# Splitting attention's weights into 16-bit planes: from VectorE to ScalarE

## The chip, the cores and the metric

The kernel runs on one core of a Trainium2 chip. A core has five engines with a queue of instructions each, which run side by side and wait for one another by semaphores: TensorE (PE, with its weight loads shown apart as PEld), VectorE (DVE), ScalarE (ACT), GpSimd (POOL) and SyncE (SP, which here only issues transfers). The metric is the device time of one execution in microseconds (us); of several executions the median is given.

## The reference

The input x holds 128 graphs of 64 nodes with 512 features in float32, and adj is one 64 x 64 mask for all of them. Four layers follow one another, each of the form x = x + f(relu(layernorm(x))):

```python
h = relu(layernorm(x)); x = x + mha0(h, adj)            # q, k, v with bias; 8 heads of 64
h = relu(layernorm(x)); x = x + mha1(h, adj) @ Wo + bo  # the same, with an output projection
h = relu(layernorm(x)); x = x + rel(h, adj)             # (adj.T * q k^T), rows scaled to norm 1, times v
h = relu(layernorm(x)); o = mha3(h, adj) @ Wp + bp      # no biases on q, k, v
x = x + o + layernorm(o) * gamma + beta
```

In mha the scores q k^T / 8 are masked, go through a softmax over the neighbours j, and weight the values. Layer 2 has no softmax.

## The kernel before

**Tiles.** 512 rows of x (8 graphs) make a tile, four blocks of 128 rows. There are 16 tiles in each layer, 64 in all, numbered n; layer l = n // 16. A tile's rows are loaded (`load_x`), normalised (`layer_norm`, line 516), and turned, so that features stand on the partitions (`hT`). The projections to q, k, v and the output are Strassen-like block products (`projection`, line 630): seven products of 256 x 256 blocks instead of eight, in the order 1, 6, 5, 2, 7, 3, 4 (line 44), where the fourth is split once more for some weights. Product 2 goes into the bank of product 1, product 7 into that of 6, product 3 into that of 5 (line 645). Sums of the inputs are made on POOL, sums of the results on POOL and DVE, and copies out of the matmul banks (PSUM, 8 of them) on ACT: the first copy of each projection is `s<-mm`, of product 1; `z<-mm` is product 5.

**Attention** of a tile (`attend`, line 813), in two halves g: after the k projection PE makes the scores (`begin_scores`), DVE adds the mask (`s`) and reduces the maximum (`mx`), POOL subtracts it, ACT takes the exponential in place, DVE sums (`sr`) and inverts, POOL multiplies. The weights are then turned, two blocks of 128 x 512 for each half, so four turns for a tile. The value products (`values`) follow while the next tile's q and k projections are under way. The last tile's weights are turned on PE instead.

**A turn** (`turn`, line 505). A float32 block [...] is split into two planes: all low halves of the 512 floats of a row, then all high halves, as 1024 uint16 (`z<-s` for attention's weights, `z<-xin` for the normalised rows; from six buffers). SP issues a transposing transfer (`hp<-z`, five buffers), and a copy on ACT puts the halves together again in their turned place (`s<-hp`, `hT<-hp`). Three places call it: line 481 for a weight (4 times), line 554 for the normalised rows (252), line 836 for attention's weights (4 for each of 47 tiles: 188). The split is on DVE (line 509), the copy back on ACT (line 514).

**The order of the work** isn't that of the program text. Every operation is recorded as a step with an engine, the steps it depends on, a duration booked by `duration` (line 265) and a delay until others see its result. `Plan.order` (line 150) then builds each engine's queue greedily: of the steps that are ready on the engine that is free first, it takes the one with the lowest rank, which is the place in the text, less 100 (`RUSH`) where the step reads a matmul bank; the score and value products come ahead. A 16-bit copy is booked at 0.67 ns for each element on DVE (line 284), after which POOL may not start until it is over, and which itself waits until POOL is free (lines 192 and 199); on ACT it is booked at 1.32 ns for each element (line 290) without regard to POOL. Each queue is issued in that order (line 217, so all instructions carry that line in the profile) and runs in order on the chip.

Of the kernel before, what the change touches and what calls it, by code (L numbers as in the profile page):

```python
# [13 lines left out]
U16 = mybir.dt.uint16  # L14
# [7 lines left out]
KC = D // P  # L22
# [279 lines left out]
def gnn_stack_kernel(  # L302
# [12 lines left out]
    pe, dve, act, gps = plan.tensor, plan.vector, plan.scalar, plan.gpsimd  # L315
# [143 lines left out]
    def fold():  # L459

        rq = yield from raw("oT", wq2, "rq")
        rk = yield from raw("SO", wk2, "rk")
        yield 4
        for dc in range(KC):
            while not mm.free:
                yield 1
            pa = mm.take("fold")
            plan.begin()
            for ec in range(KC):
                pe.matmul(pa, rq[:, ec, ts(dc, P)], rk[:, ec, :], start=(ec == 0), stop=(ec == KC - 1))  # L470
            plan.end()
            f = zs.tile([P, D], F32, tag="z", name=f"fa_{dc}")
            act.copy(f, pa)
            mm.give("fold")
            dma(a2d[dc * P : (dc + 1) * P, :], f)
            yield 1
        rv = yield from raw("oT", wv2, "rv")
        yield 4
        for ec in range(KC):
            f = zs.tile([P, KC, P], F32, tag="z", name=f"ft_{ec}")  # L480
            turn(f, rv[:, ec, :], f"v2_{ec}")
            dma(v2d.rearrange("(c p) e -> p c e", p=P)[:, :, ts(ec, P)], f)
            yield 6
# [18 lines left out]
    l_of = lambda n: n // NB  # L502
    ready = set()

    def turn(dst, src, nm):


        zp = zs.tile([P, D], F32, tag="z", name=f"zp_{nm}").bitcast(U16).rearrange("p (w f) -> p w f", w=2)
        dve.tensor_copy(zp, src.bitcast(U16).rearrange("p (f w) -> p w f", w=2))
        hp = hps.tile([P, 2, KC, P], U16, tag="hp", name=f"hp_{nm}")  # L510
        plan.sync.dma_start(
            hp.rearrange("p w c t -> p (w c) t"), zp.rearrange("p w f -> p (w f)"), transpose=True
        )
        act.copy(dst.bitcast(U16).rearrange("p c (t w) -> p w c t", w=2), hp)

    def layer_norm(n):
# [34 lines left out]
        for t in range(NT) if n else ():  # L551
            z = xins[n][t]
            act.activation(z, z, AF.Relu, bias=nb[:, t : t + 1], scale=rs[:, t : t + 1])
            turn(hT[:, :, ts(t, P)], z, f"{n}_{t}")
            yield 1
# [228 lines left out]
    def begin_scores(n, qT, kT):  # L784
        first = len(plan.steps)
        psss = scores(qT, kT, n)
        plan.join(first, 300)
        spawn(attend(n, take_scores(n, psss)))
# [24 lines left out]
    def attend(n, ss):  # L813
        for s in ss:
            sf = s.rearrange("p q b j -> p (q b) j")
            mx = sm.tile([P, NS], F32, tag="mx", name=f"mx_{n}")
            dve.tensor_reduce(mx, sf, AX.X, ALU.max)
            gps.tensor_tensor(sf, sf, mx.unsqueeze(2).to_broadcast([P, NS, G]), ALU.subtract)
            yield 1
        yield 1  # L820
        for s in ss:
            sf = s.rearrange("p q b j -> p (q b) j")
            act.activation(sf, sf, AF.Exp, scale=QS)
            sr = sm.tile([P, NS], F32, tag="sr", name=f"sr_{n}")
            dve.tensor_reduce(sr, sf, AX.X, ALU.add)
            dve.reciprocal(sr, sr)
            gps.tensor_tensor(sf, sf, sr.unsqueeze(2).to_broadcast([P, NS, G]), ALU.mult)
            yield 1

        aTs = []  # L830
        for s in ss:
            aT = s.rearrange("p (q c) b j -> p q c (b j)", q=2)
            aTs.append(aT)
            for p in range(2):
                if n < N - 1:
                    turn(aT[:, p], s[:, p * KC : (p + 1) * KC].rearrange("p c b j -> p (c b j)"), f"a_{n}_{p}")
                else:
                    pt = blocks(mm.take("last"))
                    plan.begin()
                    for c in range(KC):  # L840
                        pe.transpose(pt[:, c, :], s[:, p * KC + c].rearrange("p b j -> p (b j)"), ident)
                    plan.end()
                    act.copy(aT[:, p], pt)
                    mm.give("last")
                yield 1
        due.append((n, aTs, vs[n]))
        ready.add(("a", n))
# [410 lines left out]
    for t in range(NT):  # L1258
        ps = mm.take("last")
        plan.begin()  # L1260
        for j in range(2):
            for kc in range(KC):
                w = ((W["o3"][:, W11], w12), (W["o3"][:, W21], W["o3"][:, W22]))[kc // 2][j]
# [51 lines left out]
```

## Time and profile before

| | |
|---|---|
| median of 3 runs | 2834.38 us (2831.71 to 2835.23) |
| profiled execution | 2832.0 us, span 2829.9 us |
| PE busy | 2803.2 us, 99% |
| DVE busy | 1999.9 us, 71% |
| ACT busy | 1318.5 us, 47% |
| POOL busy | 2138.8 us, 76% |
| split of attention's weights, DVE | 188 x 1218 ns |
| split of the normalised rows, DVE | 252 x 976 ns |
| copy back to attention's weights, ACT | 188 x 1350 ns |

The span runs from the first to the last instruction of the profiled execution; the time of that execution has some 2 us more around it. A row of the groups names what is written and read (`z<-s`), the shape, the count, the busy time in all and the mean of one, and then the time for which the engine stood idle before such instructions, with what ended it. A releaser is inferred from semaphores. In the timeline a line is a start, a length and an instruction, with its idle time before in brackets; "x3" are three in a row.

### The profile page before, as it was taken

The numbers are of one execution on the slowest core, as the hardware profiler recorded it, in microseconds if no ns is written. First come the engines' busy times: TensorE is split into PE (matmuls) and PEld (weight loads), VectorE is DVE, ScalarE is ACT, GpSimd is POOL, SyncE is SP. The second block draws the span as 40 slices with busy tenths as digits, with TensorE's granted clock in tenths as the row PEclk, the third lists the DMA queues.
The fourth block names the chain that finished last, engine by engine and source line by source line (L and its number), as shares of the span: only waits on it lengthen the run. The fifth ranks groups of instructions, "written<-read, shape, count | busy, mean of one in ns | idle before, by whom it ended". The sixth has DMA issues, their size and how long they took to land.

```text
span 2829.9 us, 65896 instructions
## 1 busy us (share of the span) xinstructions
PE 2803.2 (99%) x26787; PEld 2481.2 (88%) x26787; DVE 1999.9 (71%) x3549; ACT 1318.5 (47%) x1907; POOL 2138.8 (76%) x2089
## 2 busy tenths in 40 slices
PE   9999999999999999999999999999999999999998
PEld 8888788888888888888888888888888888888887
DVE  7777667777766767767765665655588777877776
ACT  4455545445554454444543444444444444444441
POOL 6656565668898888888889655566778788788785
PEclk9999999999999999999999999999999999999999
DMA  6676556567452443443454766656656656766754
GB/s 155 133 158 148 131 152 161 114 131 165 112 128 76 105 119 77 105 120 79 106 144 114 172 156 154 160 140 164 135 113 137 145 138 141 150 135 138 161 112 117
DMA packets 645520, 375.03 MB, mean 133 GB/s; under 512 B 485728, under 2 KB 566880, under 8 KB 643296
## 3 DMA queue, kind: packets, MB, share of 16 engines
q1 hardware_dynamic: 634608, 338.32, 50.4%
q0 software_dynamic: 10608, 32.51, 6.3%
q8 instruction: 209, 3.42, 0.5%
q14 instruction: 95, 0.78, 0.1%
HBM read 152.61 MB, written 69.21 MB: 78 GB/s over the span
## 4 chain that ended last, share of the span: by engine, by line
PE 93%; POOL 3%; DMA 1%; DVE 1%; issue 1%; ACT 0%; POOLq 0%; SPq 0%; ACTq 0%; DVEq 0%
PE mm L217 93%; DMA hp<-z 1%; POOL S L217 1%; POOL w L217 1%; DMA xo<-w 0%; POOL s L217 0%; POOL xo L217 0%; POOL SO L217 0%; POOL u L217 0%; DVE xo L217 0%; DVE z L217 0%; DMA xin<-in_x_dram 0%; DVE st L217 0%; ACT s L217 0%; DVE w L217 0%
## 5 line engine op out<-in xcount | busy, mean ns | idle before, releaser
L217 PE MATMUL mm<-S,w 128*128 128x256 f32 x3584 | 812.0, 379 | 1.9 <-ACT z L217 1.9
L217 PEld LDWEIGHTS mm<-S,w 128*128 128x128 f32 x3584 | 679.3, 190 | 95.4 <-ACT z L217 2.5
L217 PE MATMUL mm<-hT,w 128*128 128x256 f32 (+1 forms) x3040 | 612.2, 347 | 2.9 <-ACT q L217 1.9
L217 PEld LDWEIGHTS mm<-hT,w 128*128 128x128 f32 x3040 | 506.9, 191 | 59.9 <-ACT q L217 2.7
L217 DVE TENSOR_TENSOR u<-mm,s 128x512 f32<-128x512 f32 x414 | 284.2, 687 | 300.9 <-PE mm L217 238.8
L217 PE MATMUL mm<-w,S 128*128 128x256 f32 x2048 | 472.4, 381 | 2.0 <-DVE u L217 2.0
L217 PEld LDWEIGHTS mm<-w,S 128*128 128x128 f32 x2048 | 384.6, 190 | 55.6 <-DVE u L217 2.4
L217 ACT COPY hT<-hp 128x1024 uint16<-128x1024 uint16 x252 | 332.5, 1351 | 49.3 <-DMA hp<-z 49.0
L217 PE MATMUL mm<-w,hT 128*128 128x256 f32 (+1 forms) x1696 | 349.2, 347 | 0.7 <-ACT s L217 0.7
L217 ACT COPY s<-hp 128x1024 uint16<-128x1024 uint16 x188 | 250.2, 1350 | 172.2 <-DMA hp<-z 109.8
L217 POOL TENSOR_TENSOR s<-s,mx 128x1024 f32<-128x1024 f32 x96 | 181.7, 1917 | 193.8 <-DVE mx L217 190.9
L217 PEld LDWEIGHTS mm<-w,hT 128*128 128x128 f32 x1696 | 285.2, 191 | 32.7 <-ACT s L217 1.1
L217 ACT COPY s<-mm 128x512 f32<-128x512 f32 x211 | 123.0, 584 | 376.3 <-PE mm L217 187.2
L217 DVE COPY z<-s 128x1024 uint16<-128x1024 uint16 x188 | 225.0, 1218 | 64.7 <-POOL s L217 64.6
L217 DVE COPY z<-xin 128x1024 uint16<-128x1024 uint16 x252 | 240.1, 976 | 20.2 <-ACT xin L217 16.7
L217 PE MATMUL mm<-w,SO 128*128 128x256 f32 x992 | 225.0, 379 | 1.0 <-POOL SO L217 1.0
L217 ACT ACTIVATE xin<-xin,nb,rs 128x512 f32<-128x512 f32 x256 | 194.5, 810 | 64.1 <-DVE nb L217 64.0
L217 POOL TENSOR_TENSOR xo<-xo,row 128x512 f32<-128x512 f32 x128 | 169.1, 1340 | 66.2 <-DMA xo<-in_x_dram 66.2
L217 PEld LDWEIGHTS mm<-w,SO 128*128 128x128 f32 x992 | 188.2, 190 | 26.9 <-POOL SO L217 1.2
L217 POOL TENSOR_TENSOR qT<-u,z 128x512 f32<-128x512 f32 x64 | 90.4, 1412 | 144.8 <-DVE u L217 124.7
L217 POOL TENSOR_TENSOR u<-u,q 128x128 f32<-128x128 f32 (+1 forms) x256 | 175.3, 693 | 30.4 <-DVE q L217 22.7
L217 POOL TENSOR_TENSOR s<-s,sr 128x1024 f32<-128x1024 f32 x96 | 188.5, 1972 | 7.7 <-DVE v L217 3.6
(125 smaller groups left out, 4245.1 us busy)
## 6 DMA issues: line engine op xcount, KB each, us to landing
xin<-x SPq DMA_DIRECT2D x192, 256.0 KB, 3.5
xo<-x SPq DMA_DIRECT2D x64, 512.0 KB, 6.1
xin<-in_x_dram SPq DMA_DIRECT2D x64, 256.0 KB, 4.2
x<-xo SPq DMA_DIRECT2D x64, 256.0 KB, 2.5
x<-xo SPq DMA_DIRECT2D x128, 128.0 KB, 2.7
x<-xo SPq DMA_DIRECT2D x32, 512.0 KB, 3.2
xo<-row POOLq DMA_DIRECT2D x16, 1024.0 KB, 8.1
out_dram<-xo SPq DMA_DIRECT2D x30, 512.0 KB, 2.8
```

What stands on the lines that cost most here:

```text
L217: getattr(getattr(self.nc, eng), op)(*a, **k)
```

## The change

`turn` gets a parameter for the operation that splits, with DVE's copy as its default. Attention's call hands in ACT's copy. The other two callers keep DVE. What the split reads and writes is the same. Since the queues are built from all booked durations, every engine's order is made anew.

```diff
-    def turn(dst, src, nm):
+    def turn(dst, src, nm, split=dve.tensor_copy):
 
 
         zp = zs.tile([P, D], F32, tag="z", name=f"zp_{nm}").bitcast(U16).rearrange("p (w f) -> p w f", w=2)
-        dve.tensor_copy(zp, src.bitcast(U16).rearrange("p (f w) -> p w f", w=2))
+        split(zp, src.bitcast(U16).rearrange("p (f w) -> p w f", w=2))
...
                 if n < N - 1:
-                    turn(aT[:, p], s[:, p * KC : (p + 1) * KC].rearrange("p c b j -> p (c b j)"), f"a_{n}_{p}")
+                    turn(aT[:, p], s[:, p * KC : (p + 1) * KC].rearrange("p c b j -> p (c b j)"), f"a_{n}_{p}", act.copy)
```

## The prediction

> **What bounds the kernel now.** I read the busy shares and the chain that ended last first, since they say which engine's time is the time.
>
> ```profile
> PE 2803.2 (99%) x26787; PEld 2481.2 (88%) x26787; DVE 1999.9 (71%) x3549; ACT 1318.5 (47%) x1907; POOL 2138.8 (76%) x2089
> PE 93%; POOL 3%; DMA 1%; DVE 1%; issue 1%; ACT 0%; POOLq 0%; SPq 0%; ACTq 0%; DVEq 0%
> ```
>
> TensorE (PE) works 2803.2 of the 2829.9 us span and is 93% of the chain. Matmul busy time alone could deceive, so I checked the floor: in the timeline eight 128x256 matmul records stand 1.73 us apart from the next eight, 216 ns each, the same in every quiet stretch. The change takes away no matmul, so those 2803.2 us stay. What can move is the 26.7 us in which PE is idle. The third view cuts the span at the places where the chain leaves PE:
>
> ```profile
> core 0: us, PE busy (x) PEld busy (x) DVE busy (x) ACT busy (x) POOL busy (x), PEclk, DMA share, GB/s
> 0.00:720.00 720.00, 715.77 (x7202) 621.34 (x7203) 520.59 (x835) 365.43 (x476) 449.79 (x348) 1.00 0.64 145
> 720.00:1470.00 750.00, 747.37 (x7264) 667.69 (x7263) 529.30 (x893) 353.63 (x539) 659.40 (x655) 1.00 0.42 104
> 1470.00:1570.00 100.00, 94.89 (x845) 83.03 (x845) 57.16 (x97) 37.59 (x56) 95.94 (x107) 1.00 0.53 133
> ...
> 2020.00:2060.00 40.00, 37.34 (x423) 32.72 (x423) 17.35 (x32) 17.00 (x25) 24.98 (x30) 1.00 0.61 118
> ...
> 2785.00:2830.00 45.00, 32.86 (x286) 28.96 (x284) 31.50 (x56) 7.36 (x14) 22.45 (x24) 0.93 0.38 94
> ```
>
> Stretch less PE busy: 4.2 us idle up to 720 (3.5 of it in the first 50 us), 2.6 at the border from layer 0 to 1, 5.1 from layer 1 to 2, 2.7 from layer 2 to 3, 12.1 at the end (span end 2829.9). The two stretches left out have none. Start and end aside, 11.1 us of PE idle can be won in the whole kernel, and POOL at 96% busy is what holds 1470 to 1570.
>
> Now the operation itself, its nearest relatives, and who waits in front of it:
>
> ```profile
> L217 ACT COPY s<-hp 128x1024 uint16<-128x1024 uint16 x188 | 250.2, 1350 | 172.2 <-DMA hp<-z 109.8
> L217 DVE COPY z<-s 128x1024 uint16<-128x1024 uint16 x188 | 225.0, 1218 | 64.7 <-POOL s L217 64.6
> L217 DVE COPY z<-s x188: 631/1042/2387, 53.5 to 2750.1; 128x1024 uint16<-128x1024 uint16 x188
> ACT z L217 <- PE mm L217: 277.0, 135, 5.1
> DVE z L217 <- POOL s L217: 64.6, 25, 4.2
> ```
>
> The split (z<-s) takes 631 ns at best and 1218 in the mean: the rest is spent inside the instruction. The last two lines are waits (us in total, times, longest): DVE stood 25 times for POOL's normalised weights, while ACT's waits are mostly for PE's own products.
>
> [...] copies of 631 ns and of 2387 ns are the same shape, and in the timeline a copy begun at 724.11 ends at 726.49, 0.6 us after POOL's multiplication (to 725.9). [...] The split on ACT isn't in this trace: I [...] take 1.35, the same engine, type and size.
>
> **The change part by part.**
>
> *Removed from DVE:* 188 copies (47 tiles x 4), 225.0 us. DVE falls from 1999.9 to about 1775 us (63%). It is not the bound, and it waits for PE 238.8 us ahead of the u adds alone, so this is worth nothing by itself.
>
> *Added to ACT:* 188 x 1.35 = 254 us; ACT rises to 1572 us (56%). In layer 0 it is densest: 365 + 64 x 1.35 = 452 of 720 us, 63%. [...] Cost at nothing in throughput: the cover is ACT's 1511 us of idle time.
>
> *The attention chain:* weights wait for split, transpose DMA, un-split on ACT, then the value products. The split gets 1.35 - 1.22 = 0.13 us longer each. In the tile around 770 us the second normalisation ends at 769.9; four ACT splits from 767.2 back to back end at 772.6, where DVE ended its fourth at 772.4. Eight ACT copies in a row would end at 778.0, 779 with the PSUM evacuations between them; before, the last un-split ended at 779.0 and PE took up the value products at 782.5. So 3.5 us of cover remains: nothing.
>
> *Evacuations behind splits on ACT:* this is the new wait. ACT is in order, and behind a split may stand the copy s<-mm or z<-mm that empties a PSUM bank. In the new order built from the changed kernel 73 of the 188 splits are followed directly by a PSUM reader, 63 by another split, 44 by an un-split, 8 by the layer norm. The cover: products 6 and 5 run between product 1 and product 2, which reuses its bank, 2 x 1.73 us; less the 0.58 us copy leaves 2.9 us of allowed delay. One split (1.35) or two (2.70) are hidden; two with a wait for POOL between them are not. I book 1 us in the whole kernel for such cases, between nothing and the rival below.
>
> [...] POOL no longer meets these copies. Layer 0 to 1 border:
>
> ```profile
> 724.11 4.90 DVE L217 COPY z<-s 128x1024 uint16<-128x1024 uint16 x3 [2.76 <-POOL s L217]
> 725.89 1.71 POOL L217 TENSOR_TENSOR v<-u,z 128x512 f32<-128x512 f32 x1
> 727.63 0.84 ACT L217 ACTIVATE z<-mm,bq 128x256 f32<-128x256 f32 x2 [4.12 <-POOL v L217]
> 728.53 1.99 PE L217 MATMUL mm<-S,w 128*128 128x256 f32 x8 [1.91 <-ACT z L217]
> ```
>
> POOL's v add takes 1.71 instead of 1.27 (the same form unhindered) under a split; ACT's z waits for it, PE for z. That is 0.44 us of the 1.91. At the 1 to 2 border, between 1501 and 1510 us, POOL runs a pair of w adds in 3.09 (free: 2.54), an xo add in 1.72, a u add and an xo add in 1.60 each (free: 1.27): 0.55 + 0.45 + 0.33 + 0.33 = 1.66 us, on the chain that holds PE there. Sum: 2.1 us won if all of it reaches PE. Elsewhere in layers 0, 1 and 3 the relief meets a PE that doesn't wait: nothing.
>
> *Moved:* the greedy planner re-sorts every queue. In the new PE order the groups that run after a later-recorded one fall from 261 to 234 of 1866 (from 43 to 30 at the 1 to 2 border, but up in layer 3, from 18, 6, 8, 6, 6, 7, 12 to 21, 10, 12, 11, 9, 13, 10 per twenty-fourth of the recorded products). On SP's queue the transposes and the next tile's xin loads swap places; xin is loaded a tile ahead, so a swap of a few 1.3 us issues is covered. The ACT instructions of the change are copies as they stand there already, and one activation table load is all the trace has, at 3.6 us. The first 65 entries of PE's order are unchanged, so the start's 3.5 us stay. At the end POOL's and DVE's lists differ by swaps of one or two instructions; the last DMA add still lands before the last four output tiles: within 1 us either way.
>
> *Sum:* +1.0 - 0.44 - 1.66 = -1.1 us. The profiled execution before took 2832.0 us (2829.9 span and 2.1 around it); that gives 2830.9. The median of the runs, 2834.38, lies 2.4 above the profiled one, so the forecast for it is 2833.3.
>
> **The rivals.**
>
> A, slower: ACT becomes a queue with a blocked head. The 25 waits for POOL's weights (64.6 us, 2.6 each, 4.2 at most) move from DVE to ACT, where every PSUM copy stands behind. 2.6 + 1.35 = 3.95 us against 2.9 of cover leaves 1.07 us of PE idle each; all 25 give 27 us, half of them 13 us: 2848. It decides from 6 of the 25 (5.7 us). For it: ACT makes the first copy of every projection, and layer 3's PE order has more late groups. Against it: DVE's u adds stood behind the same waits, and PE lost nothing outside the borders.
>
> B, faster: [...] Both vanish, 2.6 + 5.1 = 7.7 us: 2826.7. For it: POOL at 96% there, and fewer late groups in the new order. Against it: most of that 100 us is POOL's own work, which stays.
>
> C, the change does nothing because the order puts the splits on ACT only in name: excluded, all 188 stand on ACT in the built program, and VectorE's count falls by 188.
>
> **How the numbers follow.** 0.2% (5.7 us) is about what a measurement of this kernel can tell from no change. Likeliest, hidden either way, 2833.3: 0.60, its own range 2829 to 2839. A: 0.30, anywhere from 2840 to 2861, centre 2848. B: 0.10, 2824 to 2828. Faster, same, slower: 0.10, 0.60, 0.30. The range 2827 to 2850 leaves out about half of B and under half of A.
>
> **What would show it.** PE busy within 2 us of 2803; the row z<-s on ACT at 1.35 us [...]; DVE near 1775 and ACT near 1570 us; z<-xin on DVE still stretched, [...]; POOL's v, xo and w adds nearer 1.27. ACT should show a wait of z for POOL's s, some tens of us. I am wrong if PE idles outside the borders for more than 6 us with ACT's s, z or q as releaser (rival A), or if the border stalls, under 5 us together, show that B held.

## The result and the profile after

The changed kernel takes 2855.06 us (median, 2854.29 to 2855.71) against 2834.38: a ratio of 1.0074, interval 1.0057 to 1.0092. It is slower by about 21 us. The profiled execution has a span of 2853.9 us, before 2829.9.

First the busy times of after:

```profile
PE 2816.4 (99%) x26787; PEld 2490.4 (87%) x26787; DVE 1805.6 (63%) x3361; ACT 1488.2 (52%) x2095; POOL 2076.8 (73%) x2089
```

DVE gave up 194 us, POOL 62 us, ACT took 170 us. PE has the same 26787 matmuls, and yet 13.2 us more of busy time. That is the first hint: the same work took longer on an engine that the change doesn't touch. (The chain of waits is of no use here. In this execution it breaks off after 2% of the span, so I read stretches and waits instead.)

Next the same stretches as in the prediction, of after; the first column is the stretch, then its length, then the busy time and instructions of each engine, then PE's granted clock:

```profile
core 0: us, PE busy (x) PEld busy (x) DVE busy (x) ACT busy (x) POOL busy (x), PEclk, DMA share, GB/s
0.00:720.00 720.00, 717.60 (x7207) 623.69 (x7208) 458.88 (x772) 423.50 (x540) 431.83 (x352) 1.00 0.62 145
720.00:1470.00 750.00, 743.25 (x7228) 663.50 (x7228) 453.31 (x830) 407.67 (x594) 624.11 (x647) 1.00 0.42 103
1470.00:1570.00 100.00, 97.58 (x833) 85.82 (x834) 50.83 (x97) 41.07 (x63) 97.06 (x107) 1.00 0.50 136
...
2020.00:2060.00 40.00, 36.61 (x293) 32.06 (x293) 11.85 (x24) 21.49 (x30) 24.32 (x28) 0.96 0.72 127
2060.00:2785.00 725.00, 715.02 (x6943) 636.64 (x6942) 510.78 (x940) 380.80 (x543) 586.54 (x593) 0.99 0.62 135
```

Layer 3 before, where PE had no idle time at all:

```profile
2060.00:2785.00 725.00, 725.00 (x7032) 648.25 (x7031) 565.78 (x1011) 336.10 (x495) 609.89 (x607) 1.00 0.64 139
```

The border from layer 1 to 2 (1470 to 1570) has become better: 2.4 us of PE idle where there were 5.1. Layer 1 (720 to 1470) has become worse: 6.8 where there were 2.6. And layer 3 (2060 to 2785) now has 10.0 us of idle and a granted clock below 1. For the full account I took, in both traces, the time by which PE had issued the same number of matmuls. The lag of after behind before grows by 0.0 us in layer 0 and over the border behind it, by 5.9 in layer 1, by -2.9 at the border from 1 to 2, by 2.0 at the border from 2 to 3, and by some 18 us in layer 3. The last matmul ends at 2842.5 us instead of 2819.3.

Then the operation and the waits of after. A wait line is the waiting engine and tile, the releasing one, the time in all, how often, and the longest:

```profile
L217 ACT COPY z<-s 128x1024 uint16<-128x1024 uint16 x188 | 192.2, 1046 | 125.2 <-POOL s L217 125.2
L217 ACT COPY s<-hp 128x1024 uint16<-128x1024 uint16 x188 | 248.8, 1351 | 14.5 <-DMA hp<-z 13.4
...
PE mm L217 <- DVE q L217: 9.9, 4, 2.5
PE mm L217 <- DVE kT L217: 5.2, 13, 1.1
PE mm L217 <- ACT z L217: 3.1, 3, 2.0
PE mm L217 <- ACT s L217: 2.6, 2, 2.4
```

The splits do wait on ACT for POOL's weights, 125.2 us, twice what DVE waited. But PE hardly waits for ACT. It waits for DVE, the engine that was relieved: four times for a `q` and thirteen times for a `kT`.

**The four waits for `q`** stand in layer 3 at 2152, 2313, 2474 and 2635 us, one in every three tiles. Of after's timeline at the first these are the lines that matter, put in order by engine; the timelines further below show such lines alone too (start, length, instruction, idle time before it with its releaser):

```profile
2147.18 5.04 DVE L217 SCALAR_TENSOR_TENSOR xo<-z,rs,xo 128x512 f32<-128x512 f32 x3 [3.94 <-DMA xo<-kT]
2152.14 1.22 DVE L217 SCALAR_TENSOR_TENSOR nb<-mv,rs 128x4 f32<-128x4 f32 x1
2153.28 1.02 DVE L217 SCALAR_TENSOR_TENSOR xo<-z,rs,xo 128x512 f32<-128x512 f32 x1
2154.22 0.28 DVE L217 TENSOR_TENSOR q<-mm,q 128x128 f32<-128x128 f32 x1
2153.40 1.52 ACT L217 ACTIVATE xin<-xin,nb,rs 128x512 f32<-128x512 f32 x2 [5.98 <-DVE nb L217]
2154.82 0.56 ACT L217 COPY kT<-mm 128x512 f32<-128x512 f32 x1
2149.96 1.71 POOL L217 TENSOR_TENSOR SO<-oT 128x512 f32<-128x512 f32 x1
2154.56 0.94 PE L217 MATMUL mm<-hT,w 128*128 128x128 f32 x6 [2.47 <-DVE q L217]
```

`xo<-kT` is the transfer that adds the layer's output into `xo` in layer 3. DVE stands 3.94 us for it. Then its `xo<-z` run into POOL's `SO` adds: 5.04 us for three, 1.7 each, where the fastest of all 64 takes 0.73. Behind them in the same queue stand the small `nb`, for which ACT has waited 5.98 us, another `xo<-z`, and last `q`, which reads a PSUM bank that PE needs. PE stands 2.47 us. The kernel before had the same late transfer, but another order behind it. DVE's lines of its timeline at a tile of the same kind:

```profile
2192.82 1.24 DVE L217 SCALAR_TENSOR_TENSOR nb<-mv,rs 128x4 f32<-128x4 f32 x1
2196.97 1.03 DVE L217 SCALAR_TENSOR_TENSOR xo<-z,rs,xo 128x512 f32<-128x512 f32 x1 [2.91 <-DMA xo<-kT]
2197.92 0.28 DVE L217 TENSOR_TENSOR q<-mm,q 128x128 f32<-128x128 f32 x1
2198.12 1.60 DVE L217 SCALAR_TENSOR_TENSOR xo<-z,rs,xo 128x512 f32<-128x512 f32 x2
```

`nb` came ahead of the wait, and `q` behind one `xo<-z` instead of four. PE lost nothing there.

Short stretches of after at the same place show where the extra busy time of PE comes from (columns as above):

```profile
2152.00:2156.20 4.20, 1.73 (x11) 1.43 (x11) 4.20 (x7) 2.80 (x5) 4.12 (x6) 1.00 0.45 162
2156.20:2159.60 3.40, 3.40 (x9) 2.66 (x8) 2.79 (x5) 1.59 (x3) 3.30 (x3) 0.50 1.04 220
2159.60:2163.00 3.40, 3.40 (x17) 3.01 (x16) 1.22 (x3) 1.10 (x2) 0.46 (x1) 1.00 0.94 200
```

After the stall PE gets half its clock for 3.41 us (a "half clock" in what follows): 9 matmuls where the next stretch has 17. So one event costs 2.47 us of idle, 1.7 us of half speed and some 0.5 us that I can't assign, 4.7 in all; four of them are the 18 us. The stall of 2.37 us at the border from layer 2 to 3 brings the fifth half clock. Before had none of these between start and end.

**The waits for `kT`** are in layer 1, twelve alike, one in each tile:

```profile
1010.97 1.14 POOL L217 TENSOR_TENSOR u<-u,q 128x128 f32<-128x128 f32 x2
1012.15 0.48 DVE L217 SCALAR_TENSOR_TENSOR kT<-mm,bk,u 128x256 f32<-128x256 f32 x1 [0.34 <-POOL u L217]
1012.69 1.16 PE L217 MATMUL mm<-kT,qT 64*64 64x64 f32 x64 [0.34 <-DVE kT L217]
```

POOL's last small adds end just too late for `kT`, and the score products wait for that: 0.34 us each, and by the lag some 0.55 us with the restart.

### The profile page after: what moved, and what is told of

Same layout as the page of the kernel before. It is cut to its first block, busy times and chain, and to the rows that moved or that the text cites. A ratio compares the mean times of both kernels' runs of the same rounds, so it can differ in the third digit from the quotient of the medians.

```text
span 2853.9 us, 66007 instructions
## 1 busy us (share of the span) xinstructions
PE 2816.4 (99%) x26787; PEld 2490.4 (87%) x26787; DVE 1805.6 (63%) x3361; ACT 1488.2 (52%) x2095; POOL 2076.8 (73%) x2089
## 5 line engine op out<-in xcount | busy, mean ns | idle before, releaser
L217 PE MATMUL mm<-hT,w 128*128 128x256 f32 (+1 forms) x3040 | 613.0, 347 | 10.1 <-DVE q L217 9.9
L217 DVE COPY z<-xin 128x1024 uint16<-128x1024 uint16 x252 | 254.3, 1029 | 33.6 <-ACT xin L217 23.7
L217 ACT COPY z<-s 128x1024 uint16<-128x1024 uint16 x188 | 192.2, 1046 | 125.2 <-POOL s L217 125.2
L217 ACT COPY s<-hp 128x1024 uint16<-128x1024 uint16 x188 | 248.8, 1351 | 14.5 <-DMA hp<-z 13.4
L217 POOL TENSOR_TENSOR xo<-xo,row 128x512 f32<-128x512 f32 x128 | 181.6, 1437 | 59.6 <-DMA xo<-in_x_dram 59.6
L217 POOL TENSOR_TENSOR S<-hT 128x512 f32<-128x512 f32 x126 | 160.2, 1272 | 53.3 <-ACT hT L217 53.2
L217 ACT ACTIVATE s<-s 128x1024 f32<-128x1024 f32 (+1 forms) x112 | 108.1, 967 | 161.8 <-POOL s L217 84.1
```

What stands on the lines that cost most here:

```text
L217: getattr(getattr(self.nc, eng), op)(*a, **k)
```

## The experiments

**The engine and the order apart.** The change does two things: another engine executes the split, and all queues are ordered anew. The first run keeps before's order and only issues the 188 splits on ACT, in the place they had (`swap` holds their numbers):

```diff
+            if i in self.swap:
+                eng, calls = "scalar", [("copy", *calls[0][1:])]
```

> Every queue in the order that was planned with the splits on DVE, but the 188 splits of attention's weights are issued on ACT, at the same places of that order. Theory O (the new order costs the time, the engine doesn't): like the kernel before, 2831 to 2838 us, PE idle near 27 us, no PE stall over 2 us in layer 3. Theory E (the work on ACT itself costs the time): near the changed kernel, 2850 to 2860 us, with PE waiting for ACT's s, z or q.

Measured: 2834.41 us, ratio 1.0007 (0.9999 to 1.0015). Its busy line and PE's largest wait:

```profile
PE 2806.3 (99%) x26787; PEld 2483.4 (88%) x26787; DVE 1785.6 (63%) x3361; ACT 1489.6 (53%) x2095; POOL 2076.3 (73%) x2089
...
PE mm L219 <- ACT s L219: 3.6, 5, 1.0
```

DVE, ACT and POOL carry within 20 us what they carry in after, and the loss isn't there: layer 3 has 1.7 us of PE idle and no half clock. The split on ACT by itself makes no difference that can be told; the interval reaches from nothing to 4 us. The second run is the other half, after's order with the splits issued on DVE:

```diff
+            if i in self.swap:
+                eng, calls = "vector", [("tensor_copy", *calls[0][1:])]
```

> Every queue in the order that was planned with the splits on ACT, but the splits are issued on DVE. Theory O: slow as the changed kernel or slower, 2852 to 2862 us, with the four stalls of 2.5 us in layer 3 from DVE q still there. Theory E: near the kernel before, 2832 to 2840 us.

Measured: 2909.8 us, 1.0274 (1.026 to 1.0288), far worse than I had expected. PE's waits:

```profile
PE mm L219 <- DVE kT L219: 24.8, 15, 2.0
PE mm L219 <- DVE q L219: 11.8, 7, 2.7
```

The same two waits, larger. Engine and order don't add up; my reading, not tried, is that the new order leaves no room on DVE for splits that it places on ACT. What the two runs show is that the loss sits in the new order; that it sits in DVE's part of it is read from the waits here and tried further below.

**The booking of the late transfer.** In DVE's new queue the `xo<-z` stand at once ahead of `q` because the plan believes them done by then. It books the accumulating transfer at 1.1 us of issue and 2000 + size/150 ns, so 10.1 us for 1 MB; the page of after has

```profile
xo<-kT POOLq DMA_DIRECT2D x14, 1024.0 KB, 13.5
```

from issue to landing. This run is after with 3.4 us more for it:

```diff
-        return 1100, 2000 + size / 150
+        return 1100, 5400 + size / 150
```

> The changed kernel, with the accumulating transfer xo<-kT booked 3.4 us longer in the planner (it lands 13.5 us after its issue; the planner counts on some 10). Theory O with this cause (DVE stands at xo<-z for a late transfer while q, which PE waits for, stands behind): the four stalls of layer 3 go, 18 us of them with the half clock after each, 2833 to 2840 us. If the late transfer isn't the cause, the stalls stay or others take their place: 2850 to 2860 us.

Measured: 2835.62 us, 1.0013 (1.0007 to 1.002). Layer 3, the group behind the transfer, and PE's largest wait in this run:

```profile
2060.00:2785.00 725.00, 724.05 (x7147) 647.46 (x7146) 537.41 (x956) 384.69 (x550) 604.09 (x606) 1.00 0.62 139
...
L217 DVE SCALAR_TENSOR_TENSOR xo<-z,rs,xo 128x512 f32<-128x512 f32 x64 | 61.9, 987 | 3.1 <-DMA xo<-kT 3.0
...
PE mm L217 <- DVE kT L217: 5.6, 13, 1.2
```

DVE waits 3.0 us for the transfer instead of 50.4 in after, layer 3 has 0.9 us of idle instead of 10.0, its clock is 1.00, and by the two ratios 17 us are back. What remains is layer 1's `kT`, untouched as it should be. One booked number decided layer 3's loss, most of the whole. It does so by way of the order: all queues are sorted anew, and in most tiles of layer 3 `q` now stands ahead of all `xo<-z`.

**The change in two layers only.** The splits go to ACT in layers 0 and 1 and stay on DVE behind them:

```diff
-                    turn(aT[:, p], s[:, p * KC : (p + 1) * KC].rearrange("p c b j -> p (c b j)"), f"a_{n}_{p}", act.copy)
+                    turn(aT[:, p], s[:, p * KC : (p + 1) * KC].rearrange("p c b j -> p (c b j)"), f"a_{n}_{p}", act.copy if n < 2 * NB else dve.tensor_copy)
```

> The splits on ACT in layers 0 and 1 alone, on DVE in layer 3, order planned anew; DVE's order around xo<-z in layer 3 is then that of the kernel before. Theory O: layer 3 loses nothing, layer 1 loses some 6 us in twelve small waits for kT, the border to layer 2 gives some 3 back: 2835 to 2841 us. Theory E: two thirds of the loss of 21 us stay, 2848 us.

Measured: 2836.95 us, 1.0016 (1.001 to 1.0023). Layer 1 has its 6 us of loss, the border from 1 to 2 its 3 us of gain, as in after. In layer 3 DVE's order is before's again, and PE is idle for 0.9 of the 725 us:

```profile
2060.00:2785.00 725.00, 724.13 (x7027) 647.09 (x7026) 564.25 (x1010) 334.49 (x492) 609.98 (x606) 1.00 0.65 139
```

So the three places are independent, and layer 3's loss comes from the change there.

**Which of DVE's instructions.** Four runs take after as it is and move instructions in DVE's queue only, at the four bad places only; everything else keeps its order. In each, the plan's list is re-sorted so that the `xo<-z` named `late` come behind `q`; `run` holds the five instructions `xo, xo, xo, nb, xo`. The first two bring only `q` forward, behind the first `xo` and then ahead of the last:

```diff
+                late = run[1:]
...
+                for k, i in enumerate(late):
+                    moved[i] = at[q] + 0.01 * (k + 1)
```

```diff
+                late = run[4:]
```

> The changed kernel's own queues, with one thing moved on DVE in four tiles of layer 3: q, which stood behind xo, xo, xo, nb, xo, stands behind the first xo. If those four places are the loss: each gives back its stall of 2.5 us, the half clock after it (3.4 us at half speed, 1.7 us) and some 0.5 us of restart, 4 x 4.7 = 19 us: 2833 to 2839 us. If they are a symptom of a chain that is late anyway: 2845 to 2855 us.

> The same with q moved ahead of the last xo alone: PE then waits some 0.9 us less at each of the four places, a stall of about 1.5 us in place of 2.5. If the half clock comes from the length of the stall, it goes as well: 4 x (0.9 + 1.7) = 10.5 us less, 2842 to 2846 us. If the clock isn't caused by the stall, 4 x 0.9 = 3.8 us less: 2849 to 2853 us.

Measured: 2856.01 us, 1.0084 (1.007 to 1.0098), and 2854.27 us, 1.0079 (1.0066 to 1.0091). Neither wins anything. The timeline of the first (`q` behind the first `xo`):

```profile
2154.84 1.52 ACT L249 ACTIVATE xin<-xin,nb,rs 128x512 f32<-128x512 f32 x2 [5.99 <-DVE nb L249]
2156.26 0.56 ACT L249 COPY kT<-mm 128x512 f32<-128x512 f32 x1
2156.88 3.44 PE L249 MATMUL mm<-w,hT 128*128 128x256 f32 x8 [2.69 <-ACT kT L249]
```

PE no longer waits for `q`, but 2.69 us for ACT's `kT`, a PSUM copy that stands behind `xin`, which waits for `nb`, which stands behind the same `xo<-z`. In the second the stall falls into two, 1.53 us for `q` and 0.88 for `kT`, and three of the four places still get the half clock. So `q` was only the first of those that wait. The next two runs bring `nb` forward. Alone, behind which the first three `xo<-z` are put:

```diff
+                late = run[:3]
...
+                    moved[i] = at[run[3]] + 0.01 * (k + 1)
```

And with `q`, ahead of all four:

```diff
+                late = run[:3] + run[4:]
...
+                    moved[i] = at[q] + 0.01 * (k + 1)
```

> The same with nb alone ahead; q stays behind the four xo. nb's 1.2 us leave the block ahead of q and kT is on time, so a stall of some 1.3 us for q is left: 2838 to 2849 us. With the stalls as they were: 2854 us.

> The changed kernel's own queues; in the same four tiles of layer 3 DVE gets nb and q ahead of all four xo. Moving q alone won nothing: PE then waited 2.7 us for ACT's kT copy, which stands behind xin, which waits for nb, which stood behind the xo. If those two ways, q and nb, are the whole of it: the four stalls and their half clocks go, 4 x 4.7 = 19 us: 2833 to 2840 us. If a third follower of the late transfer takes over: 2848 to 2856 us.

Measured: 2855.27 us, 1.008 (1.0066 to 1.0094), and 2844.7 us, 1.0039 (1.0027 to 1.0052). With `nb` alone PE still waits 2.08 us for `q` at each place, and three of the four get the half clock. With both, no place does, and 10 us are back; a third instruction shows, in this timeline of the last run:

```profile
2147.35 6.25 DVE L249 SCALAR_TENSOR_TENSOR xo<-z,rs,xo 128x512 f32<-128x512 f32 x4
2154.39 0.68 DVE L249 TENSOR_TENSOR u<-mm,s 128x512 f32<-128x512 f32 x1
2155.13 3.72 PE L249 MATMUL mm<-w,S 128*128 128x256 f32 x16 [0.95 <-DVE u L249]
```

The four `xo<-z` take 6.25 us together, 1.56 each, while POOL adds beside them, and now `u` is late by 0.95 us. What follows: the cause is the whole block of `xo<-z`, begun late. That POOL's adds stretch it is read from the durations and wasn't tried by itself. What reads PSUM behind the block on DVE (`q`, `u`), or on ACT behind DVE's `nb` (`kT`), made PE wait in turn; a better order inside the block recovers about half.

**All that is misbooked.** In after POOL's small adds are booked at 2.41 ns an element (308 ns for 128) and take 457, and the split on ACT is booked at 1.32 ns an element and takes 1.02. The next run corrects these and the transfer together, with POOL's values fitted to the durations in the trace; the run after it gives the same bookings for transfer and POOL to the kernel before, splits on DVE.

```diff
-        return n * (1.82 if n > D else 2.41), 120
+        return (40 + 1.82 * n if n > D else 187 + 2.12 * n), 120
...
-        return 1100, 2000 + size / 150
+        return 1100, 5400 + size / 150
...
-        return max(240 + 0.49 * n, (1.32 if out.dtype == U16 else 1.4 if own else 0.95) * n), 170
+        return max(240 + 0.49 * n, (1.02 if out.tensor.name.startswith("z_") and out.dtype == U16 else 1.32 if out.dtype == U16 else 1.4 if own else 0.95) * n), 170
```

> The changed kernel, planned with durations as the traces have them: the accumulating transfer 3.4 us longer, POOL's adds at 187 + 2.12 ns for each element (457 and 727 ns for 128 and 256 elements, booked before at 308 and 617), the split on ACT at 1045 ns (booked 1352). If the rest of the loss is wrong booking too, the twelve waits for kT in layer 1 (6 us) go and the layer 3 stalls stay away: 2826 to 2833 us. If a new order brings new stalls as often as it takes some: 2833 to 2850 us.

> The kernel before, with the same corrected bookings for the transfer and for POOL's adds; the splits stay on DVE. Theory O (an order is as good as its bookings): like the kernel before or up to 6 us faster, 2827 to 2834 us. If the kernel before is good by the luck of its order, slower: 2836 to 2860 us.

Measured: 2830.48 us, 0.9992 (0.9984 to 1.0001), with the splits on ACT; 2856.13 us, 1.0084 (1.007 to 1.0098), with the splits on DVE. Layer 1 in the former, and layer 3 in the former and then in the latter:

```profile
720.00:1470.00 750.00, 748.96 (x7268) 667.88 (x7267) 445.68 (x832) 405.23 (x601) 630.44 (x651) 1.00 0.43 104
...
2060.00:2785.00 725.00, 724.88 (x7034) 649.39 (x7033) 518.61 (x956) 381.69 (x552) 593.31 (x605) 1.00 0.62 138
```

```profile
2060.00:2785.00 725.00, 709.86 (x6713) 626.40 (x6705) 590.71 (x981) 324.61 (x484) 601.03 (x588) 1.00 0.62 133
```

With truer bookings both losses of after are gone. The same bookings make the kernel before 23 us worse; PE stalls 15.1 us in its layer 3, in many pieces. So before's 2832 to 2834 us owed something to an order that suited the chip better than the plan knew, and with these bookings the kernel with splits on ACT is 25.6 us faster than the one with splits on DVE. That isn't the worth of the engine: the run with splits on DVE still books them at 686 ns and any wait for POOL, where they took 1218 in the mean before, so its plan stays wrong in the operation that the other run has right. I didn't take the three corrections apart beyond the transfer's own run, so which of them mends layer 1 (POOL's adds are the likely one) is argued only.

**A version that is faster.** The borders remained: PE stalls of 2.85 us at 1525 and 2.74 us at 2051, each with a half clock. The last run keeps all three corrections and puts every split on ACT, those of the 252 normalised rows and the weights' four too:

```diff
-    def turn(dst, src, nm, split=dve.tensor_copy):
+    def turn(dst, src, nm, split=act.copy):
```

> The corrected bookings of all_booked, and the splits of the normalised rows (252) and of the four weight blocks on ACT as well. If what ACT takes off DVE [...] is worth time once the order is planned with true durations: faster than all_booked, 2818 to 2828 us. If ACT, then some 60% busy, delays the evacuations: 2831 to 2850 us.

Measured: 2824.09 us, 0.9968 (0.9955 to 0.998). It beats both kernels. Its busy times and the border from layer 1 to 2:

```profile
PE 2803.0 (99%) x26787; PEld 2484.3 (88%) x26787; DVE 1585.9 (56%) x3105; ACT 1740.4 (62%) x2351; POOL 2018.1 (72%) x2089
...
1470.00:1570.00 100.00, 100.00 (x896) 89.20 (x895) 47.22 (x101) 52.12 (x73) 91.70 (x108) 1.00 0.58 149
```

The span is 2821.8 us, 8.1 less than before's. The borders from 1 to 2 and from 2 to 3 have no PE idle at all, where before had 5.1 and 2.7: 7.8 us, about the whole gain. Whether the borders are free because no split stands on DVE beside POOL's adds any more, or only by another order, this one run doesn't tell.

## Why the prediction was wrong, by its steps

I forecast 2833.3 us and no measurable change, with 2827 to 2850 as the range; it took 2855.06.

*What bounds the kernel*: PE, and the floor of its busy time, held, but with a gap. I took 2803.2 us as fixed, since no matmul is taken away. PE was busy for 2816.4: five half clocks of 3.41 us give 8.5 us of the difference; the rest I can't assign. I had priced a stall at its own length. Here a stall of 2.4 us with its half clock costs over 4.

*Removed from DVE*: right that it was worth nothing that can be told by itself (before's order with ACT: 1.0007). DVE fell to 1806 us in after, 1786 in before's order, near my 1775; most of the rest is its own operations, stretched: `xo<-z` 1042 ns in the mean instead of 900, and `z<-xin` 1029 instead of 976 (675 at best), still stretched as I said.

*Added to ACT*: hidden, as I said. The size was off: 1046 ns a split, not 1350, so 192 us and not 254. I took it from the row of the copy back (`s<-hp`, same engine, type and size), which still has 1351 in after; the float32 exponential of that size on ACT, 1058 in the trace of before, was the nearer row. The split and the copy back differ in where they step: the split reads 16-bit elements two apart and writes them side by side, the copy back writes them two apart. That this is the reason wasn't tried. Alike in engine, type and size wasn't alike enough. It changed nothing in the result.

*The attention chain* and *Evacuations behind splits on ACT*: both hidden. PE waits for ACT's `s` and `z` 5.7 us in the whole of after. I booked 1 us for the evacuations. One place comes near it, at the border from layer 2 to 3, in this timeline of after:

```profile
2031.08 1.35 ACT L217 COPY s<-hp 128x1024 uint16<-128x1024 uint16 x1 [4.12 <-DMA hp<-z]
2032.30 1.04 ACT L217 COPY z<-s 128x1024 uint16<-128x1024 uint16 x1
2040.19 1.14 PE L217 MATMUL mm<-s,v 64*64 64x64 f32 x32 [2.37 <-ACT s L217]
```

A split stands behind a copy back that waits 4.12 us for its transfer, and the value products behind that split's own copy back start 2.37 us late (before: 1.50). That would be the blocked head of ACT's queue, with a split as the one that suffers. The border costs 2.0 us. A split on ACT alone doesn't bring it about: in before's order with the splits on ACT no stall there is longer than 1.2 us, and with layer 3's splits back on DVE the same stall is 1.24 us, both without a half clock. So here too it takes the new order; that the split's place is the cause is read from the order of starts.

*Given back on POOL*: right there, wrong on what it is worth in the end. POOL's relief is real, 62 us. The run in before's order with the splits on ACT shows it by itself. At the border from 0 to 1 PE's stall fell from 1.91 to 1.47 us, just the 0.44 that I booked, and the next stall grew from 0.73 to 1.34. At the border from 1 to 2 the adds fell to 1.27 to 1.29 and PE's idle by 1.3 us where I booked 1.66, and then a stall of 1.94 us brought a half clock that a stall of 1.96 at that place hadn't brought before (the last part shows what went with that). So the chains are longer than the one add, and the sum is nothing. In after the adds at the border from 1 to 2 fell from 1.72 and 1.60 to 1.27 and 1.28 too, and 2.9 us came back, but there the order is another one as well. At the border from 0 to 1 nothing came back. The timeline of after there:

```profile
720.16 3.76 POOL L217 TENSOR_TENSOR s<-s,sr 128x1024 f32<-128x1024 f32 x2
723.88 1.26 POOL L217 TENSOR_TENSOR v<-u,z 128x512 f32<-128x512 f32 x1
726.06 2.00 PE L217 MATMUL mm<-S,w 128*128 128x256 f32 x8 [1.96 <-ACT z L217]
```

`v` takes 1.26 instead of 1.71 us, but it begins behind POOL's own two normalisations. PE stands 1.96 us, before 1.91.

*Moved*: this is the step that failed. I wrote that the planner re-sorts every queue, counted how many late PE groups there were, saw that they rise in layer 3, and then followed only SP's queue and the end of POOL's and DVE's. I booked the re-sorting at nothing. It cost 18 us in layer 3 and 6 in layer 1. DVE's queue in layer 3 was the one to read. The order built from the changed kernel already showed `xo, xo, xo, nb, xo, q` in the four tiles where before had `xo, q, xo, xo`, and the waits of before had the row that makes it dear:

```profile
DVE xo L217 <- DMA xo<-kT: 44.2, 13, 4.6
```

DVE waits 44.2 us in all, at 13 of the 14 transfers, which land 13.6 us after their issue and are booked at 10.1.

*Rival A* had the right sign, its 2840 to 2861 holds the time, and its mechanism fell. The waits for POOL's weights moved to ACT and doubled (64.6 to 125.2 us), and PE didn't care: before's order with the splits on ACT lost nothing that can be told. I had said that I'd be wrong if PE idled over 6 us outside the borders with ACT's `s`, `z` or `q` as releaser. It idled, with DVE's `q` and `kT` as releasers. *Rival B*, with PE's idle time of 2.6 us at the border from layer 0 to 1 and of 5.1 from 1 to 2 gone, doesn't hold for this change. The last experiment comes near its picture: it has none at the border from 1 to 2, and 1.3 us in the stretch with the border from 0 to 1.

Two things stay open: why the bad order falls on every third tile, and what in the order of layer 1 puts POOL's adds 0.34 us too late.

## What to carry to other kernels

Where queues are built from booked durations, as here, taking work off an engine that isn't the bound can change the order more than the load: run the new engine in the old order to see the two apart. Before booking a re-sorting at nothing, find the longest wait on the relieved engine's queue, compare what the plan books for it with the trace, and list what reads PSUM behind it. And price a stall of PE at its length plus the half clock that it may bring: in these traces stalls from 1.94 us on could bring one, 3.41 us at half speed.

## What the hardware showed

**The clock after a stall.** In after the five half clocks before the end last 3.41 us each. They cost about half of that: with `nb` alone brought forward, by PE's lag behind the kernel before, the place without one cost 2.4 us and those with one 4.0 each. The stalls that brought one on are all five of 2.37 to 2.48 us in after, three of four of 2.69 (`q` behind the first `xo`), three of four of 2.08 (`nb` alone), one of 1.94 in before's order with ACT; others of 1.9 to 2.3 us brought none. So in these traces the length of the stall doesn't decide alone: 1.94 us were enough at times and 2.69 not always. Where the stall falls goes with it too. The segments of granted clock between after's half clocks last 112.64, 157.01, 157.01 and 157.01 us, which is 33 and three times 46 times 3.413 us, so its half clocks begin on one grid of 3.413 us. Nine traces have more than one stretch of half clock, and in each all of them begin on such a grid. Cut along its grid, after's five stalls leave PE idle for 2.29, 1.80, 2.43, 2.48 and 2.03 us within one step of the grid, and the half clock begins where that step ends; the stall of 1.96 us at 724, with 1.88 in one step, brought none. Counted in this way over the 13 traces, up to 2790 us and outside the half clocks themselves, all 24 steps in which PE is idle for 1.97 us or more are followed by a half clock, none of the 51 with 1.0 to 1.8 us, and 5 of the 13 between. The stall of 2.69 us that brought none is split by the end of a step into 1.96 and 0.73. What sets the grid isn't shown.

**DVE beside POOL's adds.** `xo<-z` took 0.73 us at best and 1.7 back to back with POOL's adds, and `nb`, 4 elements a row, 1.22 us where the fastest took 0.10. Beside a queue of POOL's adds of 1.3 to 1.7 us, instructions of both sizes took about as long as one of these adds. What holds them isn't shown.
